# Cross attention with image prompts: the keys' two chunks as seven block products in batches 3, 5 and 7

## The chip, the cores and the metric

The kernel runs on one core of a Trainium2 chip. Its time is the device time of one execution in microseconds. All data are 32-bit floats. Five engines of the core work side by side, each through its own row of instructions: TensorE (PE in the profile; its weight loads are PEld), VectorE (DVE), ScalarE (ACT), GpSimd (POOL) and SyncE (SP), which only issues transfers. ACT and POOL issue transfers too, from their own rows.

## What is computed

Eight batches, 112 queries of 320 channels (20 heads of 16), 375 context tokens of 512 channels: 371 text tokens and 4 prompt tokens. Cut to what matters:

```python
q, k_t, v_t = heads(x @ W_q), heads(text @ W_k), heads(text @ W_v)
probs_t  = softmax(q k_t^T * 0.25)                  # over 371 text tokens
text_out = probs_t v_t
scores   = q k_ip^T * 0.25                          # 4 prompt tokens, own W_k_ip
qsem     = l2norm(probs_t @ text)                   # 512 wide, per head
sem      = qsem . l2norm(prompt)
probs_ip = softmax(scores + 0.5 * sem) * spatial_mask
out      = (text_out + probs_ip v_ip) @ W_out + b_out + x
```

The kernel never forms probs @ text. It takes its length from the context's gram matrix, ctx ctxT, and so multiplies the probabilities by one matrix u that holds the gram rows and the values side by side.

## The kernel before

**A batch.** The context is loaded (ct), transposed by DVE in three pieces of 128 tokens (ctxT, L452), and POOL copies the four prompt columns behind the third piece (L440). From ctxT, TensorE makes the gram (ps_g, L533), which goes through ug into u by transfers on SP (L547); the keys kT in two chunks of 128 channels (ps_k, L563: four products of 371 columns each) and a last one of 64 channels in two token halves (last_keys, L580); and the values vext in three chunks of 128 tokens. In batches 2 to 7 two of the value chunks are made by seven block products instead of eight (two_chunks, L663), from sums of token blocks (xs, L639 to L642) and of weight blocks (wvt), with seven adds on POOL (L667). The third chunk is an ordinary product (ps_v, L605). The values go to DRAM (vd, L684 and L699), come back by head (vr, L708, on SP), and POOL copies them into u group by group (placed, L755).

**A group.** A batch has five groups of four heads. Per group: scores (ps_s, L789), their largest on DVE, exponentials on ACT (L806), the probabilities to groups of 32 by a transfer on SP (xg, L813), transposes on DVE (L825), the products with u in twelve blocks (ps_qd, L837) and the reductions on DVE (L890). At a batch's end the attention is put together, transposed on TensorE (ps_a, L985), copied out by ACT (aT, L989) and multiplied by W_out (ps_o, L994).

**The order.** All five engines' rows are written by hand. Groups run in pairs (`pair`), in the order (0,0), then two by two; the last batch has its own loop. Scores run two groups ahead of the products. Between two pairs stands a stage (`behind`) with the other work of TensorE: in even batches b after groups 0, 2 and 4, in odd ones after groups 1 and 3. A generator such as `k(b)`, `v(b)`, `q(b)`, `f(b)`, `gr(b)` or `turned(b)` advances the keys, values, queries, ending, gram or context transposes of batch b by one piece. `turn` lists the PSUM pools from which the stage's banks come (qd has four, sc and mm two each). An even b's stage after group 2 makes the first key chunk, the seven value products and the first query chunk of batch b + 1; its stage after group 4 makes a second query chunk, the transposes of the attention of batch b − 1, the second key chunk of b + 1, the output product, and the gram of batch b + 2. The token sums for batch b + 1 are made in stage (b, 0), where the third value chunk is a product as well. The residual x lies in one tile, loaded in three pieces.

Of the kernel before, what the change touches and what calls it, by code (L numbers as in the profile page):

```python
# [8 lines left out]
F32 = mybir.dt.float32  # L9
# [11 lines left out]
def kernel(  # L21
# [15 lines left out]
    P = 128  # L37
# [66 lines left out]
    x_sb = const.tile([S, B, C], F32, tag="x_sb", name="x_sb")  # L104
# [12 lines left out]
    wvt = const.tile([P, 4, 2, CH], F32, tag="wvt", name="wvt")  # L117
    early = wvt.rearrange("p i k f -> p (i k f)")[:N, : 2 * E].rearrange("p (i f) -> p i f", f=E)
# [223 lines left out]
    def load_inputs(b0, b1):  # L342
        nc.gpsimd.dma_start(x_sb[:, b0:b1, :], x[b0:b1].rearrange("b s c -> s b c"))
# [212 lines left out]
    def keys(b):  # L556
# [3 lines left out]
        for i in range(FULL):  # L560
# [34 lines left out]
    def values(b):  # L595
# [6 lines left out]
        for c in range(0 if b < 2 else 2, NT):  # L602
            ps = bank(f"ps_v_{b}_{c}")
            for e in range(NE):
                nc.tensor.matmul(  # L605
                    ps[:, :C],
                    ctxT[:, e, c * P : (c + 1) * P],
                    wv_sb[:, e, :],
                    start=(e == 0),
                    stop=(e == NE - 1),  # L610
                )
            nc.scalar.copy(vext[:, c, :], ps[:, :C])
            yield
# [7 lines left out]
    def weight_sums():  # L621

        b11, b12 = wv_sb[:, LO, EARLY], wv_sb[:, LO, LATE]
        b21, b22 = wv_sb[:, HI, EARLY], wv_sb[:, HI, LATE]
        t1, t2, t3, t4 = (wvt[:, i] for i in range(4))
# [5 lines left out]
    def token_sums(b):  # L631

        x = st[b]["ctxT"]
        a11, a12 = x[:, LO, :P], x[:, HI, :P]
        a21, a22 = x[:, LO, P : 2 * P], x[:, HI, P : 2 * P]
        sums = work.tile([P, 4, 2, P], F32, tag="xs", name=f"xs_{b}", bufs=1)
        st[b]["xs"] = sums
        s1, s2, s3, s4 = (sums[:, i] for i in range(4))
# [5 lines left out]
    def two_chunks(b):  # L644
# [3 lines left out]
        s1, s2, s3, s4 = (s["xs"][:, i] for i in range(4))  # L648
        t1, t2, t3, t4 = (wvt[:, i] for i in range(4))
        a11, a12 = x[:, LO, :P], x[:, HI, :P]  # L650
        a22 = x[:, HI, P : 2 * P]
        b11, b21 = wv_sb[:, LO, EARLY], wv_sb[:, HI, EARLY]
        b22 = wv_sb[:, HI, LATE]
        p1, p5, p6, p7 = (
            work.tile([P, CH], F32, tag=f"v{n}", name=f"v{n}_{b}", bufs=1) for n in (1, 5, 6, 7)
        )
# [8 lines left out]

        def plus(to, one, other):
            nc.gpsimd.tensor_tensor(to, one, other, ALU.add)  # L667
# [16 lines left out]
    def values_to_dram(b, eng, c0=0, c1=NT):  # L684
# [7 lines left out]
        for c in range(c0, c1):  # L692
            q = 0
            while q < QN:
                p, n = DEAL[c].index(q), 1
# [560 lines left out]
    def pair(n):  # L1256
# [23 lines left out]
        if n in inputs:  # L1280
            load_inputs(*inputs[n])
# [321 lines left out]
```

## Time and profile before

| | |
|---|---|
| runs | 403.95, 405.25, 407.1 us; median 405.25 |
| the profiled execution | 405.13 us, span 403.4 |
| granted clock of TensorE | 0.999 |
| TensorE, share of the span | 99% |
| DVE, ACT, POOL | 82%, 49%, 45% |
| products with u (L837) | 216.9 us busy in 3840 matmuls |
| key chunks (L563), value block products (L663) | 43.4 us in 128; 24 outputs of 160 columns copied by ACT at 295 ns |

In the profile a busy share counts matmuls and operations, not the issuing of transfers. A row of the chain of waits has the start in us, the length in us, and the engine, tile and line of the work that ended last at that time. A row of an engine's timeline has the start, the length, the operation with its output and inputs, how many of them, and in square brackets the idle time before it and what ended that. In a row of windows the columns are the stretch and its length, then busy time and count for PE, PEld, DVE, ACT and POOL, the granted clock, the share of the DMA engines and GB/s.

### The profile page before, as it was taken

The page shows a single profiled execution, that of the slowest core. Times are in us where ns is not written, and L with a number is a line of the kernel's source. Part 1 is how long each engine was busy: PE and PEld are TensorE (multiplying, and loading weights), DVE is VectorE, ACT ScalarE, POOL GpSimd, SP SyncE. Part 2 cuts the span into 40 slices and gives each one's busy share as a digit, 9 for nine tenths or more (in the row PEclk, how much of TensorE's full clock was granted, in tenths as well). Part 3 has the DMA queues.
Part 4 walks back from the last instruction along what each step waited for, and adds up shares of the span by engine and source line. Part 5 has one row for each costly group of instructions (what it writes and reads, how often), then busy time and mean ns, then how long its engine had stood idle before and what let it go on. Part 6 is the DMA issues. An engine that isn't in the chain of part 4 may idle for free.

```text
span 403.4 us, 14380 instructions
## 1 busy us (share of the span) xinstructions
PE 398.0 (99%) x5673; PEld 321.9 (80%) x5673; DVE 331.3 (82%) x703; ACT 198.5 (49%) x707; POOL 182.7 (45%) x391
## 2 busy tenths in 40 slices
PE   8999999999999999999999999999999999999996
PEld 7867688888878787978787878877886878887894
DVE  3445789887998897987998898897798988888984
ACT  3146333337443943525653665334743485446764
POOL 7746021151571658051563338532256155704681
PEclk9999999999999999999999999999999999999999
DMA  7969846778666957567557766566746544776311
GB/s 228 215 186 225 189 130 179 207 190 184 166 172 166 220 130 185 148 161 166 155 157 165 199 165 171 160 171 152 187 126 174 131 124 117 195 172 174 107 52 28
DMA packets 58390, 65.85 MB, mean 163 GB/s; under 512 B 20165, under 2 KB 51641, under 8 KB 58324
## 3 DMA queue, kind: packets, MB, share of 16 engines
q1 hardware_dynamic: 54814, 58.23, 57.5%
q0 software_dynamic: 2336, 5.42, 5.4%
q10 hardware_dynamic: 1174, 1.29, 1.0%
q8 instruction: 45, 0.74, 0.9%
q14 instruction: 21, 0.17, 0.2%
HBM read 20.22 MB, written 5.22 MB: 63 GB/s over the span
## 4 chain that ended last, share of the span: by engine, by line
PE 97%; POOL 1%; DMA 1%; issue 0%; ACT 0%; SPq 0%; POOLq 0%
PE ps_qd L837 46%; PE ps_k L563 10%; PE ps_g L533 8%; PE ps_v L605 7%; PE ps_s L789 6%; PE ps_vs L663 6%; PE ps_q L394 3%; PE ps_o L994 3%; PE ps_k L580 3%; PE ps_g L495 1%; DMA ct<-in_ctx_dram 1%; PE ps_a L985 1%; PE ps_q L376 1%; PE ps_c L464 0%; POOL attn L980 0%; PE ps_o L1086 0%
## 5 line engine op out<-in xcount | busy, mean ns | idle before, releaser
L837 PE MATMUL ps_qd<-u,xgT 32*112 32x40 f32 (+11 forms) x3840 | 216.9, 352 | 0.2
L837 PEld LDWEIGHTS ps_qd<-u,xgT 32*112 32x112 f32 x3840 | 179.6, 172 | 32.0 <-issue 4.8
L825 DVE STREAM_TRANSPOSE xgT<-xg 128x768 f32<-128x768 f32 (+1 forms) x63 | 123.2, 1974 | 6.6 <-DMA xg<-p 5.9
L806 ACT ACTIVATE p<-ps_s,nmx 112x371 f32<-112x371 f32 x160 | 85.5, 585 | 63.2 <-DVE nmx L802 62.1
L802 DVE TENSOR_REDUCE nmx<-ps_s 112x1 f32<-112x371 f32 x160 | 76.7, 532 | 23.9 <-PE ps_s L789 22.5
L755 POOL COPY u<-vr 128x64 f32<-128x64 f32 x120 | 27.0, 237 | 152.4 <-PE ps_qd L837 82.8
L890 DVE CUSTOM_DVE_ANT_0 p<-ps_qd,p 112x371 f32<-112x371 f32 x152 | 73.5, 541 | 11.7 <-ACT pvs L864 7.4
L789 PE MATMUL ps_s<-kT,qm 32*112 32x375 f32 (+1 forms) x320 | 61.3, 485 | 0.0
L864 ACT COPY pvs<-ps_qd 112x21 f32<-112x21 f32 x152 | 21.8, 200 | 55.6 <-DVE ss L890 49.8
L563 PE MATMUL ps_k<-ctxT,wk_sb 128*128 128x371 f32 x128 | 43.4, 482 | 0.0
L563 PEld LDWEIGHTS ps_k<-ctxT,wk_sb 128*128 128x128 f32 x128 | 23.1, 190 | 12.8 <-issue 0.8
L533 PE MATMUL ps_g<-ctxT 128*32 128x119 f32 (+11 forms) x672 | 32.7, 338 | 0.0
L533 PEld LDWEIGHTS ps_g<-ctxT 128*32 128x32 f32 x672 | 27.7, 109 | 6.1 <-POOL xs L639 1.3
L789 PEld LDWEIGHTS ps_s<-kT,qm 32*112 32x112 f32 x320 | 27.6, 171 | 6.1 <-POOL vext L667 1.1
L605 PE MATMUL ps_v<-wv_sb,ctxT 128*128 128x320 f32 x96 | 28.3, 441 | 0.0
L452 DVE STREAM_TRANSPOSE ctxT<-ct 128x512 f32<-128x512 f32 x21 | 22.5, 1084 | 5.0 <-DMA u<-ug 5.0
L808 ACT COPY ipl<-ps_s 112x4 f32<-112x4 f32 x140 | 24.3, 174 | 0.0
L605 PEld LDWEIGHTS ps_v<-wv_sb,ctxT 128*128 128x128 f32 x96 | 17.5, 190 | 6.6
L570 ACT COPY kT<-ps_k 128x371 f32<-128x371 f32 x16 | 7.5, 469 | 23.1 <-PE ps_k L563 23.1
L973 POOL TENSOR_TENSOR vip<-vip,w 112x1280 f32<-112x1280 f32 (+1 forms) x8 | 17.5, 2185 | 0.2 <-DVE w L967 0.2
L517 POOL TENSOR_TENSOR ug<-ug,half 128x128 f32<-128x128 f32 (+1 forms) x24 | 10.6, 450 | 14.9 <-ACT ug L516 12.8
L512 ACT ACTIVATE ug<-ps_g 128x279 f32<-128x279 f32 (+5 forms) x24 | 8.0, 333 | 18.3 <-DMA ct<-in_ctx_dram 7.8
(179 smaller groups left out, 441.5 us busy)
## 6 DMA issues: line engine op xcount, KB each, us to landing
xg<-p SPq DMA_DIRECT2D x159, 162.3 KB
u<-ug SPq DMA_DIRECT2D x120, 99.0 KB
ct<-in_ctx_dram SPq DMA_DIRECT2D x28, 176.0 KB
vip<-vipd SPq DMA_DIRECT2D x7, 560.0 KB
vr<-vd SPq DMA_DIRECT2D x20, 120.0 KB
out_dram<-ob SPq DMA_DIRECT2D x7, 140.0 KB
vr<-vd SPq DMA_DIRECT2D x12, 80.0 KB
x_in<-in_x_dram POOLq DMA_DIRECT2D x12, 70.0 KB, 3.7
```

What stands on the lines that cost most here:

```text
L533: nc.tensor.matmul(ps[p * RG : (p + 1) * RG, s0 : T - t0], ctxT[:, e, t0 + q * RG : t0 + (q + 1) * RG], ctxT[:, e, t0 + s0 : T], start=(e ...
L563: nc.tensor.matmul(ps[:, :TT], wk_sb[:, e, i * P : (i + 1) * P], s["ctxT"][:, e, :TT], start=(e == 0), stop=(e == NE - 1),)
L605: nc.tensor.matmul(ps[:, :C], ctxT[:, e, c * P : (c + 1) * P], wv_sb[:, e, :], start=(e == 0), stop=(e == NE - 1),)
L663: nc.tensor.matmul(ps[:, :CH], a[:, k], t[:, k], start=(k == 0), stop=(k == 1))
L755: nc.gpsimd.tensor_copy(region(b, c)[:, :, UV - c * P :], s["vr"][:, c * QN : (c + 1) * QN, g, :])
L789: nc.tensor.matmul(ps[:S, :w], qm[a * RG : (a + 1) * RG, i, r, j * S : (j + 1) * S], s["kT"][a * RG : (a + 1) * RG, i, :w], start=True, st ...
L802: nc.vector.tensor_reduce(nmx, ps[:S, :TT], AX.X, ALU.max, negate=True)
L806: nc.scalar.activation(p, ps[:S, :TT], AF.Exp, bias=nmx)
L808: nc.scalar.copy(s["ipl"][:, groups[g][a], :], ps[:S, TT:T])
L825: nc.vector.transpose(xT[:, j : j + n].rearrange("p j (k q) -> p q j k", q=QN), xg[:, :, j * RG : (j + n) * RG].rearrange("p q (j k) -> p ...
L837: nc.tensor.matmul(banks[a][:S, j * RG : UW], xT[a * RG : (a + 1) * RG, j, :S], region(b, c)[a * RG : (a + 1) * RG, p, q * RG :], start=(j ...
L890: nc.vector.tensor_tensor_reduce(out=p, in0=ps[:S, :TT], in1=p, scale=1.0, scalar=0.0, op0=ALU.mult, op1=ALU.add, accum_out=s["ss"][:, h : ...
```

## The change

In batches 3, 5 and 7 (`seven(b)`) both key chunks come from seven block products (`two_halves`): the tokens in halves of 192 and 179, the embedding in halves, the two chunks as halves of the channels. The token sums are made once, 192 instead of 128 wide, and used for keys and values. The values' two block chunks therefore cover tokens 64 to 191 and 256 to 383, and the third chunk is tokens 0 to 63 and 192 to 255, as two halves of 64 in one bank (16 matmuls for 8). `DEALT` maps these to the rows of vd: three transfers for the third chunk, issued by ACT in stage (b, 0) (before: two by POOL in stage (b, 2)), and five for the others, by POOL (before: four). The sums of the key weights (wkt) are made on POOL in stage (1, 1). Stage (b, 2), b even, now runs q, then both key chunks, then the value products; stage (b, 4) has no key chunk. Two context transposes move from the pair before stage (b, 4) into stage (b, 2). The residual is loaded batch by batch into a ring of three tiles. In odd batches the first transfers vd to vr move from the pair to the start of stage (b, 3).

```diff
+    wkt = const.tile([P, 4, 2, P], F32, tag="wkt", name="wkt")
...
+    def load_inputs(b):
+        own_inputs[b] = work.tile([S, C], F32, tag="xo", name=f"xo_{b}", bufs=3)
+        nc.gpsimd.dma_start(own_inputs[b], x[b])
...
-        for i in range(FULL):
+        if seven(b):
+            two_halves(b)
+            yield
+        for i in range(0 if not seven(b) else FULL, FULL):
...
+            m = HALF - P if seven(b) else P
             for e in range(NE):
...
+                for h in range(P // m):
+                    t0 = h * HALF if seven(b) else c * P
+                    nc.tensor.matmul(
+                        ps[h * m : (h + 1) * m, :C],
+                        ctxT[:, e, t0 : t0 + m],
...
+    HALF = TP // 2
+    DEALT = ((2, 3, 4, 5), (8, 9, 10, 11), (0, 1, 6, 7))
+    def seven(b):
+        return b > 2 and b % 2 == 1
...
-        a11, a12 = x[:, LO, :P], x[:, HI, :P]
-        a21, a22 = x[:, LO, P : 2 * P], x[:, HI, P : 2 * P]
+        w = HALF if seven(b) else P
+        a11, a12 = x[:, LO, :w], x[:, HI, :w]
+        a21, a22 = x[:, LO, w : 2 * w], x[:, HI, w : 2 * w]
...
+    def two_halves(b):
...
+        a11, a12, a22 = x[:, LO, :HALF], x[:, HI, :HALF], x[:, HI, HALF:TT]
+        b11, b21, b22 = wk_sb[:, LO, :P], wk_sb[:, HI, :P], wk_sb[:, HI, P : 2 * P]
+        c11, c12 = kT[:, 0, :HALF], kT[:, 1, :HALF]
+        c21, c22 = kT[:, 0, HALF:TT], kT[:, 1, HALF:TT]
+        def times(a, t, to):
+            ps = bank(f"ps_ks_{b}")
+            w = min(to.shape[-1], a.shape[-1])
+            for k in range(2):
+                nc.tensor.matmul(ps[:, :w], t[:, k], a[:, k], start=(k == 0), stop=(k == 1))
+            nc.scalar.copy(to, ps[:, :w])
...
+            blocks = DEALT[c] if seven(b) else range(c * QN, (c + 1) * QN)
+            to = [(i // QN) * P + DEAL[i // QN].index(i % QN) * RG for i in blocks]
...
-    inputs = {5: (0, 2), 9: (2, 5), 19: (5, B)}
+    inputs = {5 + 5 * b - b % 2: b for b in range(B - 2)} | {31: B - 2, 33: B - 1}
...
-        if g > 1 and g != 2:
+        if g > 2 and (b % 2 or b == 0):
             turned(b + 2)
...
-        if one in ((b, 2), (b, 3)):
+        if one == (b, 2) or one == (b, 3) and (b % 2 or b == 0):
             turned(b + 2, 1 + (one == (0, 3)))
...
-            if g == 2:
-                values_to_groups(nb, 0, 2)
...
+                values_to_dram(nb, nc.scalar, 2)
                 tr(1)
...
-            turn[:] = ["qd"] * (8 if b else 3) + ["mm"]
+            turn[:] = ["qd"] * 12 + ["sc", "mm", "mm"] if b else ["qd"] * 3 + ["mm"]
...
-                values_to_dram(nb, nc.gpsimd, 2)
+                q(nb)
                 k(nb)
                 tr(0)
+                turned(b + 2)
                 v(nb)
-                q(nb)
+                turned(b + 2)
                 values_to_dram(nb, nc.gpsimd, 0, 2)
...
-            k(nb)
+            if b == 0:
+                k(nb)
             tr(0)
...
+            if b == 1:
+                weight_sums(wk_sb, wkt, P)
         else:
             turn[:] = ["qd"] * 3 + ["sc"]
+            values_to_groups(nb, 0, 2)
```

`seven_products` holds what stood in `two_chunks`: seven `times`, each followed by the adds that it completes; ACT copies each product out and POOL makes seven adds. `with_bias` reads the batch's own tile.

On TensorE, the stage after group 2 of batch 2, where ps_k, ps_ks are keys of batch 3, ps_vs its values, ps_q queries. Before:

```order
L563 MATMUL ps_k_0_2253<-ctxT_1583,wk_sb 128x371 x4
L663 MATMUL ps_vs_2265<-wv_sb,ctxT_1583 128x160 x2
L663 MATMUL ps_vs_2269<-wvt,xs_1933 128x160 x2
L663 MATMUL ps_vs_2274<-wvt,xs_1933 128x160 x2
L663 MATMUL ps_vs_2278<-wvt,xs_1933 128x160 x2
L663 MATMUL ps_vs_2285<-wv_sb,ctxT_1583 128x160 x2
L663 MATMUL ps_vs_2290<-wv_sb,xs_1933 128x160 x2
L663 MATMUL ps_vs_2295<-wvt,ctxT_1583 128x160 x2
L394 MATMUL ps_q_0_2301<-xT_2155,wq_sb 128x224 x3
```

and after:

```order
L397 MATMUL ps_q_0_2264<-xT_2168,wq_sb 128x224 x3
L703 MATMUL ps_ks_2275<-ctxT_1584,wk_sb 128x192 x2
L703 MATMUL ps_ks_2279<-xs_1939,wkt 128x192 x2
L703 MATMUL ps_ks_2284<-xs_1939,wkt 128x192 x2
L703 MATMUL ps_ks_2288<-xs_1939,wkt 128x192 x2
L703 MATMUL ps_ks_2295<-ctxT_1584,wk_sb 128x192 x2
L703 MATMUL ps_ks_2300<-xs_1939,wk_sb 128x192 x2
L703 MATMUL ps_ks_2305<-ctxT_1584,wkt 128x179 x2
L679 MATMUL ps_vs_2326<-wv_sb,ctxT_1584 128x160 x2
L679 MATMUL ps_vs_2330<-wvt,xs_1939 128x160 x2
L679 MATMUL ps_vs_2335<-wvt,xs_1939 128x160 x2
L679 MATMUL ps_vs_2339<-wvt,xs_1939 128x160 x2
```

The query chunk has moved to the front, and seven key products of two matmuls have taken the place of the one key chunk; four more value products follow, as before.

On TensorE, the stage after group 4 of batch 2, where ps_q is a second query chunk, ps_a and ps_o belong to the ending of batch 1, ps_k_1 is the second key chunk of batch 3, and ps_g the gram of batch 4. Before:

```order
L394 MATMUL ps_q_1_2524<-xT_2155,wq_sb 128x224 x3
L985 MATMUL ps_a_2530<-ident,attn_145 128x112 x3
L563 MATMUL ps_k_1_2536<-ctxT_1583,wk_sb 128x371 x4
L994 MATMUL ps_o_2544<-wo_sb,aT_2534 112x320 x3
L533 MATMUL ps_g_0_2548<-ctxT_2414 32x375
L533 MATMUL ps_g_0_2548<-ctxT_2414 32x343
```

and after:

```order
L397 MATMUL ps_q_1_2569<-xT_2168,wq_sb 128x224 x3
L1044 MATMUL ps_a_2575<-ident,attn_145 128x112 x3
L1053 MATMUL ps_o_2583<-wo_sb,aT_2579 112x320 x3
L536 MATMUL ps_g_0_2587<-ctxT_2312 32x375
L536 MATMUL ps_g_0_2587<-ctxT_2312 32x343
L536 MATMUL ps_g_0_2587<-ctxT_2312 32x311
```

The four products of ps_k_1, which stood between ps_a and ps_o, are gone, and the rest has closed up.

On POOL, from the stage after group 2 of batch 2 to the stage after group 4, where v and vext are the block products of batch 3, u_975 belongs to batch 2, u_1586 (u_1587 after) and vr to batch 3, and ctxT_2414 (ctxT_2312 after) to batch 4. Before:

```order
L699 DMA vd_1585<-vext_2012 64x320 x2
L554 COPY kT_1584<-kip 128x3x4
L667 TENSOR_TENSOR v_3_2263<-v_3_2263,v_3_2261 128x160
...
L667 TENSOR_TENSOR vext_2012<-vext_2012,v_3_2264 128x160
L699 DMA vd_1585<-vext_2012 128x320
L699 DMA vd_1585<-vext_2012 32x320
L699 DMA vd_1585<-vext_2012 64x320
L699 DMA vd_1585<-vext_2012 32x320
L755 COPY u_975<-vr_976 128x4x16 x3
L755 COPY u_1586<-vr_1587 128x4x16 x3
L440 COPY ctxT_2414<-ipnT 128x4x4
```

and after:

```order
L557 COPY kT_1585<-kip 128x3x4
L725 TENSOR_TENSOR v_3_2273<-v_3_2273,v_3_2271 128x192
...
L725 TENSOR_TENSOR kT_1585<-kT_1585,v_3_2274 128x179
L725 TENSOR_TENSOR v_3_2324<-v_3_2324,v_3_2322 128x160
...
L725 TENSOR_TENSOR vext_2018<-vext_2018,v_3_2325 128x160
L758 DMA vd_1586<-vext_2018 64x320
L758 DMA vd_1586<-vext_2018 32x320 x2
L758 DMA vd_1586<-vext_2018 64x320 x2
L814 COPY u_975<-vr_976 128x4x16 x3
L814 COPY u_1587<-vr_1588 128x4x16 x3
L443 COPY ctxT_2312<-ipnT 128x4x4
```

Seven adds for the keys (L725, 192 and 179 wide) now stand ahead of those for the values, the two stores of vext ahead of them have gone to ACT, and the copies into u, the last three of which read vr of batch 3, still stand ahead of the prompt copy.

More of the change, by code (lines that the diff above doesn't have):

```diff
@@ L101 @@
     prologue.enter_context(tc.manual_schedule())
-    x_sb = const.tile([S, B, C], F32, tag="x_sb", name="x_sb")
     XW = C // QN
@@ L647, in two_chunks @@
         x, vext = s["ctxT"], s["vext"]
-        s1, s2, s3, s4 = (s["xs"][:, i] for i in range(4))
+        w = HALF if seven(b) else P
+        one, two = slice(w - P, w), slice(2 * w - P, 2 * w)
+        s1, s2, s3, s4 = (s["xs"][:, i, :, one] for i in range(4))
         t1, t2, t3, t4 = (wvt[:, i] for i in range(4))
-        a11, a12 = x[:, LO, :P], x[:, HI, :P]
-        a22 = x[:, HI, P : 2 * P]
+        a11, a12 = x[:, LO, one], x[:, HI, one]
+        a22 = x[:, HI, two]
         b11, b21 = wv_sb[:, LO, EARLY], wv_sb[:, HI, EARLY]
         b22 = wv_sb[:, HI, LATE]
-        p1, p5, p6, p7 = (
-            work.tile([P, CH], F32, tag=f"v{n}", name=f"v{n}_{b}", bufs=1) for n in (1, 5, 6, 7)
-        )
         c11, c12 = vext[:, 0, EARLY], vext[:, 0, LATE]
@@ L1177 @@
     nc.gpsimd.tensor_copy(wq_sb[:, :, C:], wq_sb[:, :, FULL * P : C])
-    weight_sums()
+    weight_sums(wv_sb, wvt, CH)
     run(("q", 0), lambda: project_queries(pairs[0]))
```

68 lines of the change are left out of this document (43 added, 25 removed).

## Prediction

> **What bounds the kernel now.** I read the page first: its heading, the busy shares and the chain of waits by engine.
>
> ```profile
> span 403.4 us, 14380 instructions
> PE 398.0 (99%) x5673; PEld 321.9 (80%) x5673; DVE 331.3 (82%) x703; ACT 198.5 (49%) x707; POOL 182.7 (45%) x391
> PE 97%; POOL 1%; DMA 1%; issue 0%; ACT 0%; SPq 0%; POOLq 0%
> ```
>
> TensorE is busy for 99% of the span and is 97% of the chain: what shortens its own row of work shortens the kernel, as long as no new wait opens in that row. So I read the chain in order of time through the two stages of batch 2 that the change rewrites. The columns are start, length, engine, tile and line. The first piece of products ends the list, as the start of the next pair of groups.
>
> ```profile
> 151.03 2.69 PE ps_k L563 x8
> 153.72 3.80 PE ps_vs L663 x28
> 157.53 1.14 PE ps_q L394 x6
> 158.66 1.17 PE ps_qd L837 x9
> ...
> 169.39 1.33 PE ps_q L394 x6
> 170.73 0.29 PE ps_a L985 x3
> 171.02 2.51 PE ps_k L563 x8
> 173.53 1.62 PE ps_o L994 x6
> 175.14 4.58 PE ps_g L533 x68
> ```
>
> No gap lies between the pieces. The stage after group 2 takes 2.69 + 3.80 + 1.14 = 7.63 us, and the pair behind it starts at S = 158.66. The stage after group 4 starts at S + 10.73. All times below are counted from such an S, because the pair of groups itself is not edited. What the other engines finish inside the second stage without holding TensorE up, I read from their timelines (start, length, engine, line, operation):
>
> ```profile
> 161.95 3.63 SPq L813 DMA_DIRECT2D xg<-p  x4
> 165.63 2.48 SPq L547 DMA_DIRECT2D u<-ug  x4
> 168.35 2.61 SPq L708 DMA_DIRECT2D vr<-vd  x4
> 173.42 0.59 POOL L755 COPY u<-vr 128x64 f32<-128x64 f32 x3 [8.22 <-DMA xg<-p]
> 173.95 0.20 POOL L440 COPY ctxT<-ipnT 128x16 f32<-128x16 f32 x1
> 171.05 0.44 ACT L989 COPY aT<-ps_a 128x336 f32<-128x336 f32 x1 [0.35 <-PE ps_a L985]
> ```
>
> SP issues three transfers back to back. The last issue of vr ends at 170.96, and POOL's three placed copies of vr can start 2.46 us later. Behind them in POOL's queue stands the copy of the prompt tokens into ctxT, done at 174.15, which the gram needs, and the gram starts at 175.14. ACT's copy of the attention is done at 171.49, and the output product reads it. Both waits lie today under the second key chunk, 171.02 to 173.53.
>
> **The change, part by part.** All sums stand against the profiled execution, 405.13 us (span 403.4 and 1.7 around it); the median of the three runs is 405.25, so no correction is made.
>
> *A. Seven block products instead of eight.* The price of a matmul of 192 columns isn't in the trace. It lies between 160 columns, 3.80 / 28 = 0.136 us, and 371 columns, 2.51 / 8 = 0.314 us. On the straight line between them 192 columns take 0.163 and 179 take 0.152 us. So 24 x 0.163 + 4 x 0.152 = 4.52 us for both chunks, where 16 wide ones took 2.51 + 2.51 = 5.02. The stage after group 2 becomes q 1.33 (the first query chunk, at its other place) + 4.52 + 3.80 = 9.65, which is 2.02 more than 7.63; the stage after group 4 loses 2.51. As matmuls alone that is −0.49 in each of batches 2, 4 and 6, −1.5 us in all. The bounds of one piece are 0.136 (28 pieces in 3.80, −2.2 us in all) and 0.190 (5.32, +2.4), the latter being the weight load of this row:
>
> ```profile
> L663 PEld LDWEIGHTS ps_vs<-wvt,xs 128*128 128x128 f32 x72 | 10.1, 190 | 0.0
> ```
>
> That is 28 loads of 190 ns, 5.3 us, in a stretch of 3.80 us: loads of this kind overlap matmuls here. The Trainium skill says otherwise (TensorE: Matmul & The Clock Gate, Part 3: Packing small matmuls — row/col tiling): a weight load overlaps a running matmul only if it goes to another row group. By that rule, 12 more loads in each of three stages would lie bare; the row speaks against it. It comes back as a rival.
>
> *B. What the removed chunk covered.* This decides. On TensorE the stage after group 4 loses its second key chunk, and nothing takes its place (the rows stand with the change, above). The output product (ps_o) now stands right behind the transposes (ps_a) whose copy by ACT it reads, and the gram (ps_g) 1.62 us behind that. On POOL the prompt copy (L443, L440 before) still stands behind the copies that wait for vr, and vr behind the same two transfers on SP. So it ends at S + 15.49 as now (174.15 − 158.66). The output product can start once aT is done, at S + 12.87 with ACT's copy unchanged, and ends at 12.87 + 1.62 = S + 14.49. There TensorE waits for POOL until S + 15.49, plus a hand-over of some 0.05. The gram started at S + 16.48 before; so the stage gives back 0.94, not 2.51, and batch 2 nets 2.02 − 0.94 = +1.08. Batch 4, whose pair starts at 253.67:
>
> ```profile
> 253.67 1.17 PE ps_qd L837 x9
> 270.15 4.58 PE ps_g L533 x68
> ...
> 269.22 0.20 POOL L440 COPY ctxT<-ipnT 128x16 f32<-128x16 f32 x1
> ```
>
> The prompt copy ends at 269.42 = S + 15.75, the gram started at S + 16.48: 0.68 back with the hand-over, net +1.34. Batch 6 has no gram in this place, so only the wait for aT counts:
>
> ```profile
> 361.24 2.51 PE ps_k L563 x8
> 363.75 1.61 PE ps_o L994 x6
> 365.36 1.15 PE ps_qd L837 x10
> ...
> 361.65 0.44 ACT L989 COPY aT<-ps_a 128x336 f32<-128x336 f32 x1
> ```
>
> aT is done at 362.09, the output product would end 1.61 later at 363.70 (plus the hand-over, some 0.08) where it ended at 365.36: 1.58 back, net +0.44. Sum of A and B: 1.08 + 1.34 + 0.44 = **+2.86 us**. Bounds: −1.5 if everything that the chunk covered comes earlier by itself, and +6.1 (3 x 2.02) if nothing is given back.
>
> *C. The third value chunk in 64-token halves.* Eight matmuls of 320 columns become 16 in pairs that fill the two halves of a bank. The nearest rows:
>
> ```profile
> 132.05 1.40 PE ps_k L580 x14
> 137.98 2.35 PE ps_v L605 x8
> ```
>
> The last key chunk has 16 such halves (14 in the list) of 186 columns in 1.40 us: 88 ns a piece, less than the 136 ns that 160 columns take by themselves. So two halves run side by side, and I take 0. If they didn't, it would be up to +2.35 a stage; a gain of 0.2 is the other end.
>
> *D. POOL and ACT in the rewritten stages.* On POOL seven key adds and a fifth store stand ahead of the placed copy for the pair's second group. Today:
>
> ```profile
> 158.05 1.48 POOL L667 TENSOR_TENSOR vext<-vext,v 128x160 f32<-128x160 f32 x3
> 159.48 2.09 POOL L699 DMA_DIRECT2D vd<-vext  x4
> 161.96 0.24 POOL L755 COPY u<-vr 128x64 f32<-128x64 f32 x1 [0.40 <-PE ps_qd L837]
> L837 PE MATMUL ps_qd<-u,xgT 32*112 32x392 f32 x2 | 0.5, 497 | 0.0
> ```
>
> The last adds end 2.0 us after the last value product (159.53 against 157.53). With q moved ahead, that product ends at S, so the adds end at S + 2.0, five issues of 0.52 at S + 4.6, and the copy at S + 4.85. It is needed by the second group's first wide product: the last row, from the stretch 163.5 to 163.8, none before it, so about S + 5.0. The margin is 0.15 us: I take 0. A gain is excluded, since TensorE doesn't wait there now; the upper bound is +1.0 in each of three stages (seven adds of 0.5 that are only in part hidden). ACT issues three stores ahead of the exponentials of the stage after group 0, about 1.9 us by POOL's 0.52 to ACT's 0.64 (2.54 for four):
>
> ```profile
> 60.66 2.54 ACTq L699 DMA_DIRECT2D vd<-vext  x4
> ```
>
> The exponentials behind them are due only as their score banks are needed again, and ACT is busy for 49% of the span: 0, up to +0.5 a stage. Wider token sums (384 for 256 columns), the residual's load per batch and the two context transposes that move to the earlier stage lie on POOL and DVE under the products: 0, with DVE (82% busy) up to +0.3.
>
> *E. Weight sums for the keys.* Four POOL operations of 256 columns after the stores of the stage after batch 1's group 1:
>
> ```profile
> 103.79 1.15 PE ps_qd L837 x10
> ...
> 104.31 1.49 POOL L667 TENSOR_TENSOR vext<-vext,v 128x160 f32<-128x160 f32 x3
> 107.03 0.24 POOL L755 COPY u<-vr 128x64 f32<-128x64 f32 x1 [1.23 <-PE ps_qd L837]
> L642 POOL TENSOR_TENSOR xs<-ctxT,xs 128x256 f32<-128x256 f32 x6 | 4.4, 738 | 0.0
> ```
>
> The adds end at 105.80; 4 x 0.74 = 2.95 more is 108.75, and the copy of 0.24 ends at 108.99. By D's count it is needed 5.0 after the pair's start at 103.79, near 108.8: +0.2 (0 to +0.5), once.
>
> *F. vr after xg in the odd batches.* Batch 5's stage and pair is longer than batch 3's by 18.00 − 17.47 = 0.53:
>
> ```profile
> 209.59:227.06 17.47, 17.47 (x236) 13.13 (x237) 15.87 (x31) 6.96 (x30) 6.61 (x16) 1.00 0.76 177
> 304.60:322.60 18.00, 18.00 (x236) 13.70 (x237) 15.89 (x31) 7.04 (x30) 5.68 (x15) 1.00 0.58 149
> 302.85 3.15 SPq L708 DMA_DIRECT2D vr<-vd  x4
> ```
>
> There vr is issued ahead of xg and holds the queue for 3.15 us; moved behind it, it frees xg. I take −0.3, from 0 to −0.53.
>
> **Sum**: 2.86 + 0.2 − 0.3 = +2.76; 405.13 + 2.76 = **407.9 us**, +0.7%.
>
> **Rivals.** *The cover was not needed* (R1): if vr's landing or POOL's copies come earlier, or the copy of aT is quicker, the stage gives its 2.51 back. For it: SP's transfers stand back to back only because nothing pressed them. Against it: the first begins when the exponentials are ready, which the change doesn't touch. Time: 405.13 − 1.5 − 0.1 = 403.5.
>
> *POOL comes late to the placed copy* (R2, the slower side): POOL's adds and five issues end after S + 5.0, and the second group's first product waits in each of batches 2, 4 and 6. For it: a margin of 0.15 us. Against it: POOL is 45% busy and the products wait for one copy only. It decides from the fifth issue ending after S + 4.75; at +1.0 in each stage, 407.9 + 3 = 410.9.
>
> *Weight loads lie bare, or halves run one by one* (R3): 3 x 12 x 0.19 = +6.8, or 3 x 2.35 = +7.1: about 415. The rows of A and C speak against both. (The Trainium skill's rule under A is the first of the two.)
>
> **How the numbers follow.** The forecast (406 to 409) has 0.57, R1 0.20, R2 0.19, R3 0.04. The range runs from R1's 403.5 to R2's 411.0 and leaves out R3 and the edges of the others. A measurement of this kernel can tell 1% from no change: below 401.2 or above 409.3. Faster by that needs more than twice the matmuls' own saving: 0.03, from R1's edge. Slower takes R3, most of R2 and the forecast's upper edge: 0.22. The rest, 0.75, lies within 1%.
>
> **What the profile after would show.** For A, ps_ks 28 pieces in about 4.5 us. For B, TensorE idle ahead of ps_o, released by ACT's aT, and ahead of ps_g, released by POOL's prompt copy, some 0.5 and 1.0 us in batches 2 and 4. For C, ps_v of 64 tokens, 16 pieces in about 2.35 us. For D, the placed copy's end against the second group's first wide product. For F, batch 5's stage and pair near 17.5 us. I am wrong in B if the gram starts right behind the output product, and in D if TensorE waits for L814 inside a pair.

## The result, and the profile after

| | before | after |
|---|---|---|
| runs | 403.95 to 411.04 us (6), median 405.91 | 412.07 to 416.3 us (6), median 412.14 |
| ratio of the times | | 1.0163, 95% interval 1.0129 to 1.0197 |
| profiled execution | 405.13 us, span 403.4 | 412.08 us, span 410.4 |

The ratio is taken over fast runs alone, without executions in a slower state, so it is not the quotient of the two medians. The kernel became slower by 1.6%, some 6 us, where +2.8 was forecast; 412.14 lies above the stated range. The page of the changed kernel, busy shares and chain by engine:

```profile
PE 401.1 (98%) x5733; PEld 334.8 (82%) x5733; DVE 332.1 (81%) x703; ACT 202.3 (49%) x722; POOL 200.8 (49%) x418
...
PE 79%; DMA 6%; POOL 4%; SPq 4%; ACT 2%; DVE 2%; issue 1%; POOLq 0%; DVEq 0%; ACTq 0%
```

TensorE's share of the chain fell from 97% to 79%: transfers, POOL, SP and ACT now end stretches that TensorE ended before. The view of TensorE's waits (what waited, for whom: us in total, times, the longest) lists three that the kernel before did not have:

```profile
PE ps_o L1053 <- ACT aT L1048: 2.0, 3, 0.9
...
PE ps_g L536 <- POOL ctxT L443: 1.2, 2, 0.8
PE ps_qd L896 <- POOL u L814: 0.4, 1, 0.4
```

They add up to 3.6 us. The rest doesn't appear as a wait of the matmuls in this view: TensorE is counted as busy in stretches that grew all the same. So the two executions are compared by stretches, each from the start of one of TensorE's pieces to the next (the landmarks are read from TensorE's timeline; a stage is named by its batch and group):

| stretch | before | after | difference | forecast |
|---|---|---|---|---|
| start to the value products of batch 2, in stage (1,1) | 99.82 | 100.12 | +0.30 | 0 |
| from there to stage (1,3) | 14.59 | 15.31 | +0.72 | +0.2 (E) |
| (1,3) to (2,0) | 17.57 | 18.21 | +0.64 | 0 |
| (2,0) to (2,2) | 18.98 | 19.59 | +0.61 | 0 (D) |
| (2,2) to (3,1): the two rewritten stages | 40.02 | 41.36 | +1.34 | +1.08 (A, B) |
| (3,3) to (4,0) | 17.46 | 17.85 | +0.39 | 0 |
| (4,0) to (4,2) | 18.98 | 19.66 | +0.68 | 0 (D) |
| (4,2) to (5,1): rewritten | 40.02 | 40.95 | +0.93 | +1.34 (A, B) |
| (5,3) to (6,0) | 18.00 | 17.75 | −0.25 | −0.3 (F) |
| (6,0) to (6,2) | 18.98 | 18.94 | −0.04 | 0 (D) |
| (6,2) to the last keys of batch 7: rewritten | 32.92 | 34.53 | +1.61 | +0.44 (A, B) |
| (3,1) to (3,3), (5,1) to (5,3), the end | 66.06 | 66.13 | +0.07 | 0 |

The differences add up to the 7.0 us between the spans. The rewritten stretches hold 3.9 of them, the stretches behind the stages after group 0 1.25, those behind the odd batches' stages after group 3 0.8, and the first two rows 1.0. The chain through batch 2's two stages, as shown of the kernel before:

```profile
153.30 1.33 PE ps_q L397 x6
154.63 4.51 PE ps_ks L703 x28
159.14 3.80 PE ps_vs L679 x28
...
162.94 1.15 PE ps_qd L896 x10
...
177.89 0.59 POOL u L814 x3
178.49 0.15 POOL ctxT L443
...
178.68 4.65 PE ps_g L536 x68
```

The seven key products take 4.51 us, and the pair starts at S = 162.94 with nothing between. In the second stage the chain leaves TensorE: POOL's copies into u and the prompt copy behind them end last, and the gram starts at S + 15.74 as soon as they are done. Before, it started at S + 16.48 with no wait, behind a key chunk of 2.51 us. In batch 4 the prompt copy releases the gram too, but there it waits 0.37 us for DVE's third context transpose, while POOL's copies of vr are done:

```profile
275.43 0.20 POOL L443 COPY ctxT<-ipnT 128x16 f32<-128x16 f32 x1 [0.37 <-DVE ctxT L455]
```

So two chains end close together in this stage, one by SP's vr and one by DVE.

### The profile page after: what moved, and what is told of

Its sections match the earlier page's. It is cut to its first block, busy times and chain, and to the rows that moved or that the text cites. A ratio compares the mean times of both kernels' runs of the same rounds, so it can differ in the third digit from the quotient of the medians.

```text
span 410.4 us, 14546 instructions
## 1 busy us (share of the span) xinstructions
PE 401.1 (98%) x5733; PEld 334.8 (82%) x5733; DVE 332.1 (81%) x703; ACT 202.3 (49%) x722; POOL 200.8 (49%) x418
## 4 chain that ended last, share of the span: by engine, by line
PE 79%; DMA 6%; POOL 4%; SPq 4%; ACT 2%; DVE 2%; issue 1%; POOLq 0%; DVEq 0%; ACTq 0%
PE ps_qd L896 36%; PE ps_g L536 8%; PE ps_k L569 6%; PE ps_v L614 6%; PE ps_s L848 5%; PE ps_vs L679 5%; PE ps_ks L703 3%; DMA vd<-vext 3%; PE ps_k L586 3%; DMA vr<-vd 2%; PE ps_q L397 2%; SPq L550 2%; PE ps_g L498 1%; PE ps_o L1053 1%; ACT p L865 1%
## 5 line engine op out<-in xcount | busy, mean ns | idle before, releaser
L896 PE MATMUL ps_qd<-u,xgT 32*112 32x136 f32 (+11 forms) x3840 | 220.2, 353 | 1.1 <-POOL u L814 0.4
L896 PEld LDWEIGHTS ps_qd<-u,xgT 32*112 32x112 f32 x3840 | 187.9, 172 | 28.8 <-issue 4.3
L848 PEld LDWEIGHTS ps_s<-kT,qm 32*112 32x112 f32 x320 | 29.0, 171 | 4.6 <-issue 0.7
L614 PE MATMUL ps_v<-wv_sb,ctxT 128*128 128x320 f32 (+1 forms) x120 | 28.2, 439 | 0.0
L569 PE MATMUL ps_k<-ctxT,wk_sb 128*128 128x371 f32 x80 | 27.1, 482 | 0.0
L614 PEld LDWEIGHTS ps_v<-wv_sb,ctxT 128*128 128x128 f32 (+1 forms) x120 | 16.4, 168 | 7.5
L569 PEld LDWEIGHTS ps_k<-ctxT,wk_sb 128*128 128x128 f32 x80 | 14.5, 190 | 8.3 <-issue 0.8
L725 POOL TENSOR_TENSOR v<-v,v 128x160 f32<-128x160 f32 (+1 forms) x27 | 14.8, 549 | 6.3 <-ACT v L704 3.9
```

What stands on the lines that cost most here:

```text
L569: nc.tensor.matmul(ps[:, :TT], wk_sb[:, e, i * P : (i + 1) * P], s["ctxT"][:, e, :TT], start=(e == 0), stop=(e == NE - 1),)
L614: nc.tensor.matmul(ps[h * m : (h + 1) * m, :C], ctxT[:, e, t0 : t0 + m], wv_sb[:, e, :], start=(e == 0), stop=(e == NE - 1),)
L848: nc.tensor.matmul(ps[:S, :w], qm[a * RG : (a + 1) * RG, i, r, j * S : (j + 1) * S], s["kT"][a * RG : (a + 1) * RG, i, :w], start=True, st ...
L896: nc.tensor.matmul(banks[a][:S, j * RG : UW], xT[a * RG : (a + 1) * RG, j, :S], region(b, c)[a * RG : (a + 1) * RG, p, q * RG :], start=(j ...
```

## The experiments

Three theories stood after the result. **Theory 1**: the chunk that was taken out of the stage after group 4 had covered waits there, so most of its time isn't given back. **Theory 2**: the loss lies in what else was moved: the stores on ACT, vr on SP, the weight sums on POOL. **Theory 3**: the seven products are dear in themselves.

### The chunk alone: chunk_moved

```diff
 # the kernel before, stage after group 2 of batches 2, 4, 6
-                k(nb)
+                k(nb, 2)
 # stage after group 4
-            k(nb)
+            if b == 0:
+                k(nb)
```

(In batch 6 the line goes as well, and the lists of banks follow.)

> The kernel before, with nothing added: only the second ordinary key chunk (four products, 2.51 us) of batches 3, 5 and 7 moves from the stage after group 4 to the stage after group 2, where the change has its keys. Theory 1 (the chunk was cover): the stage after group 2 grows by 2.51 each time; the stage after group 4 gives back only 0.94, 0.68 and about 1.0, as far as ACT's copy of the attention, POOL's prompt copy and the copies into u allow, and batch 7 loses 0.46 more: +5.3 us, about 411. Theory 2 (the loss lies in what else was moved: stores, vr, weight sums) and theory 3 (the seven products themselves are dear): 0, the time before.

Measured: 412.5 us beside 406.23, ratio 1.0158 (1.0108 to 1.0207). Nothing was added to this kernel. The chain of batch 2's two stages:

```profile
152.82 5.18 PE ps_k L563 x16
...
178.59 0.59 POOL u L755 x3
179.19 0.15 POOL ctxT L440
...
179.38 1.76 PE ps_g L533 x16
```

Both chunks now stand in the first stage (5.18 us), and the gram waits for the same POOL copies as in the changed kernel. The three rewritten stretches take 42.54, 41.77 and 35.68 us: +2.52, +1.75 and +2.76 over the kernel before, 7.0 together where 5.3 was expected. In batch 2 nothing of the 2.51 us came back: SP's four issues of u took 3.92 us there and 2.48 in the kernel before, POOL's copies behind vr came 0.9 us later, and the gram started at S + 16.43 (S = 162.95). Theory 1 holds, and theories 2 and 3 alone can't explain it. (The stretch (1,3) to (2,0) took 19.48 us in this profile, 1.9 more than before, where an xg needed 5.0 us to land; none of the moved work is there.)

### The cover put back: plain_keys

```diff
-        if seven(b):
-            two_halves(b)
-            yield
-        for i in range(0 if not seven(b) else FULL, FULL):
+        for i in range(FULL):
...
-            if b == 0:
-                k(nb)
+            k(nb)
```

> The changed kernel with ordinary keys: two chunks of four products, one in each of the two stages as before; everything else of the change stays (wider sums, value halves, three stores on ACT, vr later, weight sums made and not used). Theory 1: the cover is back, only the moves beside it cost: 0.7 + 0.6 in batch 1, 0.6 and 0.7 behind the stores on ACT, 0.4 and -0.3 in batches 3 and 5: +2.8 us, about 408.5. Theory 2 alone: all of the loss stays, 412. Theory 3 alone: back to the time before.

Measured: 409.12 beside 406.23, ratio 1.0078 (1.0044 to 1.0112). The second stage of batch 2:

```profile
172.58 0.29 PE ps_a L1041 x3
172.87 2.51 PE ps_k L566 x8
175.38 1.61 PE ps_o L1050 x6
176.99 1.06 PE ps_g L536 x9
```

With the chunk between ps_a and ps_o, no wait is left; the stretches of batches 2 and 4 take 40.17 and 40.19 us, 0.2 more than before, and batch 6's 33.27, 0.35 more. So about 3 us of the loss go with the seven products' placing, and about 3 remain without them: theory 2 has a share of its own.

### The prompt copy freed: third_early

```diff
-        if g > 2 and (b % 2 or b == 0):
+        if g > 2:
             turned(b + 2)
```

> The changed kernel, with the third context transpose and with it POOL's prompt copy of batches 4 and 6 moved from the stage after group 4 to the middle of the pair before it, so that the prompt copy no longer stands behind the copies that wait for vr. Theory 1: the gram follows the output product at once; it starts 1.1 us earlier in batch 2 and 0.7 to 1.0 in batch 4: -1.9 us against the change, about 410.2. Rival (DVE is the limit there: the transpose pushes its reductions and scores back): 0 or slower, 412 to 413.

Measured: 410.92 beside 406.23, ratio 1.0106 (1.0059 to 1.0153).

```profile
174.48 0.30 PE ps_a L1044 x3
...
174.81 0.45 ACT aT L1048
...
175.30 1.87 PE ps_o L1053 x6
177.17 0.84 PE ps_g L536 x6
```

The gram now follows the output product at once, and the stretches of batches 2 and 4 take 40.50 us each, 0.86 and 0.45 less than in the changed kernel. What is left of the wait is ACT's copy: ps_o stands 0.52 us behind the end of ps_a. The median is 1.2 us below that of the changed kernel; expected was 1.9, with 0.7 to 1.0 for batch 4, where the gain was smaller. The intervals of the two ratios overlap, so it is the trace that shows the gain, not the time. The edit moves the transpose on DVE and the copy on POOL together and doesn't tell the two chains apart.

### The moves beside it: side_undone, stores_late, vr_back, sums_late

side_undone has all three edits, the others one each:

```diff
 # stores_late: from stage (b, 0) to the start of stage (b, 2)
-                values_to_dram(nb, nc.scalar, 2)
...
+                values_to_dram(nb, nc.gpsimd, 2)
                 q(nb)
 # vr_back: from stage (b, 3) to the pair, b odd
+            if g == 2:
+                values_to_groups(nb, 0, 2)
...
-            values_to_groups(nb, 0, 2)
 # sums_late: from stage (1, 1) to stage (1, 3)
-            if b == 1:
-                weight_sums(wk_sb, wkt, P)
...
             load_turned(nc.gpsimd, pairs[(b + 3) // 2])
+            if b == 1:
+                weight_sums(wk_sb, wkt, P)
```

> The changed kernel with three moves undone: the third value chunk's stores on POOL at the start of the stage after group 2 (not on ACT), the first vr transfers back in the pair, the weight sums for the keys in POOL's idle time of the stage after batch 1's group 3. Theory 2 by the stages of the two traces: -0.65 twice, -0.6, -0.4 and +0.25, and -0.7: -2.8 us, about 409.3; what is left over the time before, 3.9 us, is theory 1's. If the three stores on POOL make the placed copy of the second group late: -1 at most.

> The changed kernel, with only the third value chunk's three stores moved from ACT to POOL, to the start of the stage after group 2. If the stores on ACT are what holds the pair behind the stage after group 0, that pair and stage go back from 19.6 to 19.0 us in batches 2 and 4: -1.3 us, about 411. If not: 412.1 and the two stretches as they are.

> The changed kernel, with only the first vr transfers of the odd batches back in the pair ahead of xg. If vr ahead of the stores and of u on SP is what holds the stage after group 3 and its pair, these go back from 18.2 and 17.85 us to 17.5 in batches 1 and 3, and batch 5's goes up from 17.75 to 18.0: -0.8 us, about 411.3. If not: no change.

> The changed kernel, with only the weight sums for the keys moved to POOL's idle time in the stage after batch 1's group 3. If POOL's late copy is what holds the stage after batch 1's group 1, the stretch from its value products to the next stage goes back from 15.2 to 14.5 us: -0.7, about 411.4. If SP's queue holds it (its xg is 1.3 us later there than before): no change.

Measured: side_undone 409.76 beside 406.23, ratio 1.0092 (1.0058 to 1.0126); stores_late 410.19, vr_back 411.41, sums_late 412.08 in one execution each, beside 406.36.

**The stores.** The two stretches behind the stage after group 0, in the changed kernel and then in stores_late, from the view by windows:

```profile
133.71:153.30 19.59, 19.59 (x337) 15.64 (x337) 17.45 (x40) 12.83 (x46) 11.92 (x16) 1.00 0.65 160
231.05:250.71 19.66, 19.66 (x337) 15.71 (x337) 17.48 (x40) 12.84 (x46) 11.84 (x16) 1.00 0.65 163
```

```profile
132.92:151.85 18.93, 18.93 (x338) 14.94 (x336) 17.27 (x40) 12.77 (x46) 11.93 (x17) 1.00 0.72 178
228.85:247.78 18.93, 18.93 (x338) 14.93 (x336) 17.28 (x40) 12.77 (x46) 11.92 (x17) 1.00 0.65 164
```

TensorE counts as busy all the time in both, and 0.7 us is gone all the same. ACT's timeline shows it, first before, then after:

```profile
142.67 0.57 ACT L806 ACTIVATE p<-ps_s,nmx 112x371 f32<-112x371 f32 x1 [0.18 <-DVE nmx L802]
```

```profile
142.90 2.54 ACTq L758 DMA_DIRECT2D vd<-vext  x3
...
145.66 0.56 ACT L865 ACTIVATE p<-ps_s,nmx 112x371 f32<-112x371 f32 x1
```

The first exponential started 2.34 us after the pair's start before (140.33) and 3.71 after it now (141.95): the three issues hold ACT for 2.54 us. The score banks that ACT frees are those into which the pair's second group multiplies, and that group starts late. A weight load of the products waits for ipl, ACT's last read of a score bank; before, no load waits at this place:

```profile
147.89 0.70 PEld L896 LDWEIGHTS ps_qd<-u,xgT 32*112 32x112 f32 x18 [0.26 <-ACT ipl L867]
```

The stores are what does it: over all profiles of this study, without stores on ACT the stretch took 18.93 to 18.99 us in 14 of 14 cases, and with them 19.40 to 19.84 in 13 of 14.

**vr.** vr_back's three stretches behind the stage after group 3 took 17.46, 18.20 and 17.69 us: −0.75, +0.35 and −0.06 against the changed kernel, where about −0.7, −0.35 and +0.25 was expected. Two more runs below bear on it.

**The sums.** In sums_late the stretch from batch 2's value products to stage (1,3) took 14.75 us for 15.31, in side_undone 14.59 as before; in the kernels that have the sums in their first place, 14.99 to 15.42. So the sums cost about 0.4 us there, through the placed copy behind them in POOL's queue, as in this chain of the changed kernel:

```profile
108.32 0.73 POOL wkt L645
109.05 0.19 POOL u L814
...
109.29 3.71 PE ps_qd L896 x46
```

The time of sums_late doesn't show it, as other stretches were longer in that execution. (chunk_moved, which has no such sums, took 15.06 in this place, so waits of another origin occur there too.)

side_undone got 2.4 us back for the 2.8 expected, but its batch 6 took 36.57 us for 34.53: the last store needed 4.4 us to land there (3.1 in the changed kernel), SP's vr, and u behind it, waited for that, and the four issues of vr took 3.45 us for 2.04. stores_late, with the stores in the same place, took 34.85, so these 2 us are not the stores' place alone; what made them stays open.

### The change and vr once more: change_again, vr_again

> The changed kernel once more, for a second profiled execution and for its time beside the next run. The stretches behind the odd batches' stage after group 3 took 18.21, 17.85 and 17.75 us in the first profile, against 17.57, 17.46 and 18.00 before, and 17.46 to 19.48 over all kernels so far, with vr at either place. If vr's place makes the difference, they are again near 18.2, 17.85 and 17.75. If they vary with the landing of transfers from one execution to the next, they are others.

> The changed kernel with the first vr transfers back in the pair, once more. The first reading gave vr's place -0.8 us (about 411.3 beside 412.1). If the three stretches only vary, the time is that of the changed kernel within 0.4 us.

Measured: change_again 412.39 beside 406.71, ratio 1.0151 (1.0114 to 1.0188); vr_again 411.12, ratio 1.0123 (1.0093 to 1.0153). The three stretches took 18.61, 17.88 and 17.88 us in the one and 17.46 in each place in the other. Over all 14 profiles they take 17.47 to 18.61 us with vr in the stage (mean 18.0, 18 cases) and 17.46 to 19.48 with vr in the pair (mean 17.8, 24 cases): the same kernel, in vr_back and vr_again, gives 18.20 and 17.46 in the same place. A cost of vr's place of about 0.2 us a stretch fits these numbers, but the spread is larger than that and the intervals of the two times overlap. That this move costs 0.8 us, as the two first traces seemed to say, is not shown.

change_again also holds the one exception among the stores. In its batch 4, ACT's three issues took 1.61 us, not 2.6, and the stretch took 18.94 us:

```profile
240.96 1.61 ACTq L758 DMA_DIRECT2D vd<-vext  x3
```

Batch 6 had 1.57 us in all seven profiles with stores on ACT, and no loss either. Put side by side, the time of the three issues and the length of the stretch go together:

| profile, batch | three issues on ACT | stretch |
|---|---|---|
| change_again, 4 | 1.61 | 18.94 |
| sums_late, 2 | 2.36 | 19.40 |
| the change, 2 | 2.54 | 19.59 |
| the change, 4 | 2.60 | 19.66 |
| third_early, 2 | 2.76 | 19.80 |
| plain_keys, 2 | 2.80 | 19.84 |

All 14 cases of batches 2 and 4 lie within 0.02 us of one rule: 18.94 us, and what the three issues take beyond 1.9 us is lost in full (2.80 − 1.9 = 0.90; 19.84 − 18.94 = 0.90); at 1.61 nothing is lost. No case lies between 1.61 and 2.36, so 1.9 is where the rule meets 18.94 and not a limit that was measured.

The long issues go with loads that SP issues at the same time. The context loads behind the stage after group 0, in the kernel before and then in the changed one, where ACT issues from 142.90 to 145.44:

```profile
141.43 1.22 SPq L146 DMA_DIRECT2D ct<-in_ctx_dram  x4
```

```profile
143.89 2.60 SPq L146 DMA_DIRECT2D ct<-in_ctx_dram  x4
```

In batches 2 and 4 SP's four issues took 1.22 or 1.23 us in all 14 cases without stores on ACT, and 2.60 to 3.72 in all 14 with them. In batch 6, where no such load is issued, ACT's three took 1.57 each time. The issues of the two engines thus lengthen each other when they fall together; why ACT's were short once beside SP's (1.61), and those of SP long (3.72), stays open, and no run moves the loads alone.

### Putting the parts together: mended, mended_q, mended_sp

All three make the seven products for batches 3 and 5 only, undo the three moves, keep third_early's edit, and transpose the attention before the query chunk, with ACT's copy ahead of the last group's copies:

```diff
-        return b > 2 and b % 2 == 1
+        return b in (3, 5)
...
+        if b % 2 == 0 and 0 < b < B - 2 and g == NG - 1:
+            turn[:] = ["qd"]
+            f(b - 1)
         if n < len(steps) - NG - 1:
             value_sums(b, g)
```

In mended and mended_sp the first query chunk stands behind the value products again, in mended_q ahead of the keys. mended_sp has a buffer of its own for the first product of the values, and SP issues the third chunk's stores:

```diff
-            work.tile([P, HALF], F32, tag=f"v{n}", name=f"v{n}_{b}", bufs=1)[:, :w]
+            work.tile([P, w if n == 1 else HALF], F32, tag=f"v{n}_{w if n == 1 else HALF}", name=f"v{n}_{b}", bufs=1)[:, :w]
...
-                values_to_dram(nb, nc.gpsimd, 2)
+                values_to_dram(nb, nc.sync, 2)
```

> The seven products for batches 3 and 5 only (batch 7 as before), the three side moves undone, the third transpose and the prompt copy in the pair's middle, q behind the value products again, and the transposes of the attention with ACT's copy ahead of the last group's copies on ACT, then q, then the output product. Theory 1 and 2 together: no wait is left in the two stages, so each of batches 2 and 4 is shorter than before by the matmuls' own 0.5 us (39.4 to 38.9 from the start of the stage after group 2 to the next batch's second stage), batch 6 as before: -1.0 us in all, about 405 beside 406.2. Theory 3 (the products are dear in themselves): longer than before in both batches.

Measured: 406.83 beside 406.36, ratio 1.001 (0.9981 to 1.004), where some 405 was expected; the stretches of batches 2 and 4 took 40.72 and 40.61 us, longer than before. The second stage had no wait left, but the first had a new one. TensorE's timeline, and ACT's:

```profile
157.80 0.81 PE L679 MATMUL ps_vs<-wv_sb,ctxT 128*128 128x160 f32 x4 [0.58 <-ACT v L680]
```

```profile
157.45 0.77 ACT L680 COPY v<-ps_vs 128x160 f32<-128x160 f32 x3 [2.06 <-POOL kT L725]
```

ACT stands 2.06 us until POOL's key adds release a buffer that keys and values share, and TensorE stands behind ACT. In the change itself the query chunk ahead of the keys gave POOL that time.

> The kernel of the run mended, with the query chunk ahead of the key products again, as in the change. In that run's trace TensorE stands 0.8 us in the value products, since ACT's copy of one waits for a buffer that POOL's key adds still read. If that is POOL's lateness, the query chunk ahead gives it 1.3 us: the stage after group 2 takes 9.7 instead of 10.5 us, the pair behind it 10.9 instead of 10.7, so 0.6 us less in each of batches 2 and 4: about 405.6 beside 406.4, -1.2 against mended. If the shared buffers hold it in either order: no change.

> The kernel of the run mended (query chunk last), with the buffer of the first product no longer shared between keys and values, and the third chunk's three stores issued by SP instead of POOL. If POOL's lateness and the shared buffer make the 0.8 us, the stage after group 2 takes 9.5 us, the pair 10.7, and each of batches 2 and 4 is 0.9 us shorter than in mended: about 405.2. If three more issues on SP delay xg: the pair grows by up to 0.5 and eats half of it.

Measured: mended_q 406.14 beside 407.28, ratio 0.9968 (0.9938 to 0.9999); mended_sp 405.9 beside 407.28, ratio 0.9966 (0.9938 to 0.9994). The two stages of mended_sp in batch 2:

```profile
151.16 4.71 PE ps_ks L703 x28
155.87 3.80 PE ps_vs L679 x28
159.67 1.14 PE ps_q L397 x6
160.81 1.17 PE ps_qd L896 x9
...
171.54 0.44 PE ps_a L1044 x3
171.98 1.15 PE ps_q L397 x6
173.13 1.67 PE ps_o L1053 x6
174.80 1.28 PE ps_g L536 x12
```

Nothing stands between the pieces. (mended_sp changes the buffer and the stores at once, so it doesn't tell which of the two removed the wait.) Batch 2's stretch takes 39.71 us against 40.02 before, and mended_q's 39.80 and 39.82: of the 0.49 us that the matmuls save a batch, 0.2 to 0.3 arrive. (mended_sp's batch 4 took 40.43, with 11.60 us instead of 10.70 for the pair behind the gram.) Both kernels are faster than the kernel before by 0.3%, and the intervals only just exclude no difference; as the two stretches together give 0.4 us in mended_q and lose 0.1 in mended_sp, that this gain comes from the products is not shown. Theory 3 falls all the same: with the products in it, a stretch can be shorter than before once its surroundings are put right. Where the rest of the 0.49 us goes was not singled out.

## Why the prediction failed

Two terms of the sum were too small: batch 6 in B (+0.44, measured +1.61) and the stores on ACT in D (0, measured +1.29 in two batches). They make 2.5 of the 4.2 us by which the trace's +7.0 exceeds the forecast +2.76. What the experiments say of the rest stands at the end of this section.

**A held.** 4.51 us for the key products against 4.52, 1.33 for the query chunk, 9.64 us for the stage against 9.65. Weight loads didn't lie bare: the stretch with 28 loads has the length that the straight line gave, not the 5.32 of the loads in a row.

**B held in its mechanism in batches 2 and 4.** The gram of batch 2 started at S + 15.74 against S + 15.54, released by POOL's prompt copy behind the copies of vr. Batch 4's started at 275.68 − 260.35 = S + 15.33 against S + 15.80, released by the prompt copy too; but that copy waited for DVE's third context transpose, a chain that the forecast didn't follow. Nor is the chain by vr as fixed as the forecast took it: in chunk_moved it released the gram at S + 16.43. In batch 2 an earlier xg (0.6 us), longer issues of u (1.1) and shorter ones of vr (0.6) nearly cancelled, so that this term came so close is in part luck. chunk_moved shows the mechanism without any of the change's arithmetic, and plain_keys that it goes when the cover comes back. TensorE's idle time ahead of ps_o was released by aT, as foretold (0.53 us in both batches).

**B failed in size in batch 6**, +1.61 against +0.44, at the sentence "Batch 6 has no gram in this place, so only the wait for aT counts". The wait for aT is there, 0.91 us. The chain through the stretch reads:

```profile
360.33 3.12 DMA vd<-vext
...
365.60 3.58 DMA u<-ug
...
369.18 0.09 DVE ss L949
...
369.47 0.35 ACT aT L1048
...
369.87 1.87 PE ps_o L1053 x6
...
371.82 1.31 PE ps_qd L896 x10
```

The stage after group 2 grew by 2.19 instead of 2.02 and its pair by 0.2. Counted from the pair's start at 356.23, the output product then started at S + 13.6, where the forecast had 13.4, and took 1.87 for 1.61, so the products started at S + 15.6 for the forecast 15.05. They could not have come much earlier: u is issued behind vr in this batch, vr waits for the stores to land, and POOL's copies into u end at 371.61.

```profile
371.01 0.60 POOL L814 COPY u<-vr 128x64 f32<-128x64 f32 x3 [8.03 <-DMA u<-ug]
```

The removed chunk had covered this chain as well, and the forecast hadn't followed it. The chain's step from u to ss, though, is an inference that DVE's timeline doesn't bear out: the reductions ran there without a gap behind the last score maxima, and these waited for the score products:

```profile
366.42 0.99 DVE L861 TENSOR_REDUCE nmx<-ps_s 112x1 f32<-112x371 f32 x2 [0.20 <-PE ps_s L848]
```

So aT was 0.2 us late with the pair, and the copies into u ended only 0.2 us ahead of the products. The last batch's products then ran 0.4 us longer (9.53 for 9.13 us to the last keys), which I had at nothing.

**D failed at ACT.** "The exponentials behind them are due only as their score banks are needed again ...: 0, up to +0.5 a stage." The banks are needed 5.7 us into the pair (147.63 against 141.95); the stores pushed the exponentials back by 1.4 us and cost 0.61 and 0.68 us, more than the upper bound. The issue time was taken as 1.9 us, from a row where four issues took 2.54; here three took 2.54 and 2.60, beside SP's loads. By the rule of the stores above, 1.9 is also about what the exponentials can spare; that the two figures agree is chance. Neither the spread of an issue's time nor that margin was worked out, as it was for POOL.

**D's POOL term was nearly right, and R2's condition was not met.** The five stores ended at S + 4.65, where the forecast had 4.6 and R2 needed 4.75, and the first of the two copies behind them near S + 4.9, where it had 4.85:

```profile
164.96 2.63 POOL L758 DMA_DIRECT2D vd<-vext  x5
167.58 0.42 POOL L814 COPY u<-vr 128x64 f32<-128x64 f32 x2
```

Instead of 3 us in all, the pair lost 0.2 in each batch (10.93 for 10.73). It did so in plain_keys too, which has no key adds, and not in mended_sp, where the query chunk ends the stage; so it goes with value products at the end of the stage; which wait it is was not singled out.

**C held**: the 16 pieces ran in pairs, 2.30 us against 2.35.

```profile
139.64 2.30 PE ps_v L614 x16
```

**E** was +0.4 by the experiments for +0.2, inside its bounds. **F** was looked at from one side: vr was moved behind xg, but also ahead of the third chunk's stores and of u on SP. The 0.53 us from which its gain was read lie within what such a stretch differs by between two executions of one kernel (17.46 and 18.20). The expected gain of 0.3 isn't there in the mean, and a small loss is more likely; the experiments don't settle it.

**R1** fell with chunk_moved, and **R3** with A and C. Of the 7.0 us, then, 3.9 lie in the rewritten stretches, where uncovered chains end last (2.86 forecast), 1.3 are the stores on ACT (0 forecast), 0.4 the weight sums (0.2 forecast), and some 1.4 lie in stretches that vary from one execution to the next by as much. The direction and the main mechanism were right; the range was too low, as it ended at R2's price alone, with nothing for the stores on ACT and −0.1 for the sums and vr together.

## What to carry to other kernels

Where one engine is busy for 99% of the span, a piece of its work that sits behind a hand-over is also the cover of that hand-over: before moving it, follow every chain that ends in the stage it leaves (here ACT's copy, POOL's copies behind vr, DVE's transpose, and u behind vr behind the stores), and count only what remains when the next of them ends. An issue of a transfer on an engine that also computes costs that engine's time, and that time isn't constant; put issues where the work behind them has more slack than their longest time in the trace, and look at what other engines issue beside them. And the view of waits showed half of the loss: two traces are compared by stretches between landmarks, and a stretch that differs by less than it does between two executions of one kernel says nothing.

## What was not expected of the hardware

Three issues on ACT's queue took 2.36 to 2.80 us in batches 2 and 4 (13 of 14 cases), where SP issued four loads at the same time, and 1.57 in batch 6, where it didn't, for three transfers of the same size; SP's four took 1.22 us without ACT's and 2.60 to 3.72 beside them. And the stretch behind the odd batches' stage after group 3, with the same instructions on TensorE, took 17.46 us in some executions, up to 18.61 in others and once 19.48; its shortest value, 17.46 or 17.47, came back in eight kernels. The short stretches go with early issues on SP: in 13 of the 14 short cases SP had issued the last whole group's xg within 14.9 us of the stretch's start, and in 26 of the 28 others later than that. No run changes this alone, so the cause stays open.
